# A decoder layer on one core: batch inputs loaded in another step, a product between V and scores, other last steps of self-attention, the last head's output taken by batch

## The chip, the cores and the metric

The kernel runs on one core of a Trainium2 chip. The time is the device time of one execution in microseconds (us); the median of several executions is compared. The engines are named as the profile names them: PE (TensorE, with its weight loads as PEld), DVE (VectorE), ACT (ScalarE), POOL (GpSimd) and SP (SyncE, which only issues DMAs here). A name with q, such as SPq, is an engine's queue of issued work.

## What is computed

One layer of a post-norm decoder in float32, on x of 8 batches x 256 tokens x 1024 features (16 tiles of 128 tokens):

```
x = layernorm(x + self_attention(x))              # 32 heads of 32, 8 key/value heads, rope, causal
x = layernorm(x + cross_attention(x, context))    # 32 heads of 128, 8 key/value heads, rope, mask
x = layernorm(x + gate(x) * memory(x))            # the last part
# memory: top 8 of 256 slots by a router, softmax over them, values through two small matrices
# gate: from the variance of each token (and the mean over all of them) and a small gelu network
```

The gate divides log(1 + variance) by its mean over all 2048 tokens. So the last part can be finished for no token before the second layernorm's input is there for every token.

## The kernel before

**Self-attention** (`self_attention`, line 147) runs 64 steps: s = 8 b + c for batch b and group c of four heads. The order of work on PE and POOL is the written one (`manual_schedule`, line 97); for the other engines and for DMAs issued by SP and ACT the framework's planner sets an order when the kernel is built, from the written order and its own idea of when each is ready. Each queue then runs strictly in its order, so that an instruction that waits holds up all that stand behind it. A step holds:

- `scores(s + 1)` (line 258), 16 matmuls of 32 rows (L267), whose results DVE reads with the mask (L284), ACT turns into softmax weights (L289, L295) and DVE transposes in blocks (L300, L304);
- `query(s + 2)` (L208), from the batch's input xT, and the rope on DVE (L218 to L221);
- in odd steps, for two steps at a time, `weighted` (line 316): the product of the weights and V in many 32 x 32 matmuls (L333), in two halves (`False`: 96 of them, `True`: 112), then four ACT copies to sa_oT (L343). Scores and weighted use the same two pairs of "sc" banks in PSUM, so scores of the next step wait for these copies;
- one of `others(s)`: keys and values of the next batch (c from 4 to 7), or the output projection of the batch before (`project_out`, L367, c from 0 to 3), and transposes of that batch's normalised tiles (`turn`, L391, c of 5 and 6), stored to x1T in DRAM;
- in steps 4 to 59 four `products`: the keys and values of the cross-attention, which do not depend on x, are made here.

Each such product is one of seven in a Strassen-Winograd scheme (`seven`, line 720): p1, p2, p6, p5, p3, p7, p4, eight matmul instructions each (L741, or L735 for values, which are turned). They read a quarter (512 tokens) of the context, or of x1T for queries, in blocks B11, B21, T3 (loaded as B12), B22 and the differences T1, T2, T3, T4 (`load_blocks`, line 621: loads L628, differences L632 to L635). p1 reads B11, p2 B21, p6 T2, p5 T1, p3 B22, p7 T3, p4 T4. Sums of the weights for these products are made on POOL in the self-attention (L417) and pass through DRAM.

All weights, the mask, the transposed tiles and some others share nine buffers ("w4", line 105). A load into one of them waits until its last reader is done. The batch inputs xT have two buffers (`load_x`, L162).

At the end, step 61 closes the early pool and opens the buffers of the cross-attention (`xa_early`, line 598): x1T of the first quarter, tables, keys and mask are loaded, and `mask_bias` (L679) turns the mask into what is added to scores. The first queries' seven products (`self.queries`) go into steps 62 and 63, two each, and behind the loop; those of the second pair between the last output projections.

**Cross-attention** (`cross_attention`, line 1022; only PE in written order) runs 128 heads H in four quarters q: transposes of head H (L877), scores of head H + 1 (L843), output products of the previous group of four heads (`xa_out`, seven again, L947), query products, and for each pair of heads the V product for each of two batches b (`xa_weighted`, L894, copies L902). `xa_combine` (L976) adds the sevens' parts to the residual. The memory part of the quarter before is fed in piece by piece (`self.fill`): `turn`, `project` (L1226), `query_turned` (L1236), `slot_weights` (L1243 to L1269), `weights_turned` (L1274), `mixed` (L1283).

**The tail** (`tail`, line 1408) follows the last head, whose group (G = 31) takes its output the plain way, `xa_out_plain` (L1002, 8 instructions for each half of a tile, then the layer norm). The last four tiles' memory parts, the mean variance, the gates and the 16 `final` (line 1362: two matmuls L1373, gate and add with sums on DVE L1376, the mean on POOL L1380 and L1381, squares on ACT L1384, the rest of the statistics on POOL L1385 to L1387) and their `norm` (L1394 or L1396, then the store) are interleaved by hand on PE.

The loop's middle, as it decides the order on PE:

```
if s % 2:
    weighted(s, False)
elif not first:
    one()
if s % 2 == 0 and s + 1 < last:
    scores(s + 1)
...
event()
one()
if s % 2:
    weighted(s, True)
    if s + 1 < last:
        scores(s + 1)
```

`one()` emits the next product of the step, `event()` a piece of the weights' sums.

Of the kernel before, what the change touches and what calls it, by code (L numbers as in the profile page):

```python
# [8 lines left out]
F32 = mybir.dt.float32  # L9
# [3 lines left out]
ALU = mybir.AluOpType  # L13
# [31 lines left out]
W4 = 9  # L45
# [25 lines left out]
class Layer:  # L71
# [16 lines left out]
    def run(self):  # L88
        nc = self.nc
        self.ident = self.const.tile([P, P], F32, name="ident")  # L90
        make_identity(nc, self.ident)
        self.neghalf = self.const.tile([P, 1], F32, name="neghalf")
        nc.gpsimd.memset(self.neghalf, -0.5)
        self.cos = self.const.tile([P, TQ], F32, name="cos")
        self.sin = self.const.tile([P, TQ], F32, name="sin")
        self.wsums, self.kT_d, self.v_d, self.tables_d = {}, {}, {}, {}
        with self.tc.manual_schedule(engines={PE, POOL}):
            self.self_attention()
        with self.tc.manual_schedule(engines={PE}):
            self.cross_attention()  # L100
            self.tail()

# [44 lines left out]
    def self_attention(self):  # L147
# [12 lines left out]
        def load_x(b):  # L160
            xTs[b] = ep.tile([P, KC, S], F32, name="xT", bufs=2)
            nc.sync.dma_start(out=xTs[b], in_=a["xT"][b])  # L162
# [344 lines left out]
        for s in range(last):  # L507
            b, c = divmod(s, KC)
            if c == 4:
                load_residual(b)  # L510
            if c == 6 and b + 2 < B:
                load_x(b + 2)
            if s == KV_BEGIN - 2:
# [84 lines left out]
    def xa_early(self):  # L598
# [13 lines left out]
        self.load_mask(0)  # L612
        self.mask_bias()

# [5 lines left out]

    def load_blocks(self, pool, name, src):


        nc = self.nc
        xb = {}
        for block, i, j in (("B11", 0, 0), ("B21", 1, 0), ("T3", 0, 1), ("B22", 1, 1)):
            xb[block] = pool.tile([P, 4, S], F32, name=name, bufs=7)
            nc.sync.dma_start(out=xb[block], in_=src[:, 4 * i : 4 * i + 4, j * S : (j + 1) * S])  # L628
        for block in ("T1", "T2", "T4"):
            xb[block] = pool.tile([P, 4, S], F32, name=name, bufs=7)  # L630

        nc.vector.tensor_tensor(xb["T1"], xb["T3"], xb["B11"], ALU.subtract)  # L632
        nc.vector.tensor_tensor(xb["T2"], xb["B22"], xb["T1"], ALU.subtract)
        nc.gpsimd.tensor_tensor(xb["T3"], xb["B22"], xb["T3"], ALU.subtract)
        nc.vector.tensor_tensor(xb["T4"], xb["B21"], xb["T2"], ALU.subtract)  # L635
        return xb

    def load_x1T(self, q):
        self.xb[q] = self.load_blocks(self.xp, "x1T", self.x1T_d[q])

    def xa_context(self, q):

        self.load_positions(q)
        self.cb = self.load_blocks(self.hp, "ctxT", self.a["ctxT"][q])

# [376 lines left out]
    def cross_attention(self):  # L1022
# [9 lines left out]
        for H in range(XA_STEPS):  # L1032
# [27 lines left out]
            def query():  # L1060
                if queries:
                    queries.pop(0)()
# [11 lines left out]
            for b in range(NB):  # L1074
                self.xa_turned(H, b)
            if H + 1 < XA_STEPS:
                self.xa_scores(H + 1, 0)
                if not waits:
                    query()
                self.xa_scores(H + 1, 1)  # L1080
            if i < 3:
# [23 lines left out]
            if i == 3:  # L1105
                if g == 0 and q:
                    self.xa_combine(q - 1, 0, True)
                if G == NQ * XA_KV - 1:
                    self.xa_combine(q, 0, False)
                    self.xa_combine(q, 1, False)  # L1110

# [251 lines left out]
    def final(self, t, x, wvu):  # L1363
# [5 lines left out]
        for half in range(2):  # L1369
# [9 lines left out]
            )  # L1379
        nc.gpsimd.tensor_tensor(nmean, sums[:, 0:1], sums[:, 1:2], ALU.add)  # L1380
        nc.gpsimd.tensor_scalar(nmean, nmean, -1.0 / E, None, ALU.mult)  # L1381

# [24 lines left out]

    def tail(self):
        nc = self.nc
        while self.fill:  # L1410
            self.next_fill()
        q = NQ - 1
        G = NQ * XA_KV - 1
        hid = self.uni.tile([P, QT, UNC], F32, name="w4", bufs=W4)
        tiles = [self.memory_tile(q * QT + tt, hid[:, tt, :]) for tt in range(QT)]
        norms = []
# [11 lines left out]
        def part(tt, i):  # L1428
            tiles[tt][i]()

        turn, project, query_turned, slot_weights, weights_turned, mixed = range(6)
        for t in range(8, NT - QT):
            self.load_x2(t, self.sp, "acc", 4)
        for tt in range(QT):
            for half in range(2):
                self.xa_out_plain(G, half, tt)
            if tt >= 2:
                part(tt - 2, turn)

# [7 lines left out]
        for i in range(2):  # L1447
            self.auxT.append(self.uni.tile([P, NT // 2 * P], F32, name="w4", bufs=W4))
            n = (NT // 2 - (QT if i else 0)) * P
            for half in range(2):  # L1450
# [3 lines left out]
                )  # L1454
        part(0, project)
        part(2, turn)
        part(1, project)
        part(0, query_turned)
        part(3, turn)
        lv = self.mean_log_variance()  # L1460
        part(2, project)
# [4 lines left out]
        part(1, slot_weights)  # L1466
        part(2, query_turned)
        finals(1)
        part(0, weights_turned)
        part(2, slot_weights)  # L1470
        part(3, query_turned)
        finals(1)
        part(0, mixed)
        part(1, weights_turned)
        part(3, slot_weights)
        self.memory_learned(hid, range(NT - QT, NT))
        finals(1)
        part(1, mixed)
        part(2, weights_turned)
# [5 lines left out]
        self.gates(lv, NT - QT, NT)  # L1485
        finals(NT - 5)
        for norm in norms:
# [91 lines left out]
```

## Time and profile before

| | |
|---|---|
| median of 3 runs (lowest, highest) | 3517.1 us (3503.24, 3520.21) |
| profiled execution: its time, its span | 3504.15 us, 3502.4 us |
| mean granted TensorE clock | 0.982 |
| busy: PE, PEld, DVE, ACT, POOL | 97%, 70%, 60%, 34%, 29% |
| self-attention loop, 60 to 1190 us: PE busy | 1091.6 us of 1130 |
| its end, 1190 to 1240 us: PE busy | 33.95 us of 50 |
| tail, 3440 us to the end: PE, DVE, ACT busy | 35.2, 40.69, 32.85 us of 63 |

The waits view lists, for one engine, the instruction that waited, what it waited for, the us in total, how often, and the longest. A timeline row has the start, the us that the merged instructions took, engine and line, the operation, out<-in by the program's names, shapes, xcount, and in brackets the idle time before it with what ended it. A row of the stretches has the length, each engine's busy time and count (PE, PEld, DVE, ACT, POOL), PEclk (the granted clock, 1 is full), the DMA share and GB/s.

### The profile page before, as it was taken

The numbers are of one execution on the slowest core, as the hardware profiler recorded it, in microseconds if no ns is written. First come the engines' busy times: TensorE is split into PE (matmuls) and PEld (weight loads), VectorE is DVE, ScalarE is ACT, GpSimd is POOL, SyncE is SP. The second block draws the span as 40 slices with busy tenths as digits, with TensorE's granted clock in tenths as the row PEclk, the third lists the DMA queues.
The fourth block names the chain that finished last, engine by engine and source line by source line (L and its number), as shares of the span: only waits on it lengthen the run. The fifth ranks groups of instructions, "written<-read, shape, count | busy, mean of one in ns | idle before, by whom it ended". The sixth has DMA issues, their size and how long they took to land.

```text
span 3502.4 us, 71117 instructions
## 1 busy us (share of the span) xinstructions
PE 3388.1 (97%) x27811; PEld 2459.2 (70%) x27811; DVE 2113.6 (60%) x5997; ACT 1201.2 (34%) x4030; POOL 1030.2 (29%) x1385
## 2 busy tenths in 40 slices
PE   7999999999999799999999999999999999999996
PEld 5777777787777567767776667677767766766753
DVE  4655665565555555566575665666575567566666
ACT  3434333343334423333223323333332333333224
POOL 4244655565665212111122111212111112121112
PEclk9999999999999899999999999999999999999997
DMA  8567777886877545344544334544434544444442
GB/s 291 192 218 261 272 255 256 278 273 216 299 256 252 184 160 160 126 146 135 157 145 153 129 127 140 167 136 148 137 127 135 159 153 145 133 131 134 130 142 96
DMA packets 269550, 626.36 MB, mean 179 GB/s; under 512 B 28960, under 2 KB 99760, under 8 KB 268192
## 3 DMA queue, kind: packets, MB, share of 16 engines
q1 hardware_dynamic: 194672, 441.00, 38.6%
q0 software_dynamic: 50032, 154.66, 13.6%
q10 hardware_dynamic: 24512, 26.15, 2.2%
q8 instruction: 221, 3.62, 0.4%
q14 instruction: 113, 0.93, 0.1%
HBM read 526.93 MB, written 94.77 MB: 178 GB/s over the span
## 4 chain that ended last, share of the span: by engine, by line
PE 71%; POOL 8%; issue 6%; DMA 6%; DVE 6%; ACT 2%; SPq 0%; POOLq 0%; ACTq 0%; DVEq 0%
PE mm L741 23%; PE mm L947 20%; PE mm L894 7%; PE sc L843 6%; PE mm L208 4%; POOL ws L417 3%; PE mm L735 3%; PE mm L367 2%; PE mm L1226 2%; DMA xa_wo_sums<-ws 2%; DMA xa_wq_sums<-ws 2%; PE sc L333 1%; PE sc L267 1%; POOL xa_wo_sums L466 1%; PE mm L1002 1%
## 5 line engine op out<-in xcount | busy, mean ns | idle before, releaser
L741 PE MATMUL mm<-x1T,w 128*128 128x256 f32 x3584 | 851.1, 381 | 5.0 <-DMA w<-in_xa_wq 3.8
L741 PEld LDWEIGHTS mm<-x1T,w 128*128 128x128 f32 x3584 | 676.3, 190 | 190.7 <-issue 87.7
L947 PE MATMUL mm<-w,xoS 128*128 128x512 f32 x992 | 449.2, 595 | 1.2 <-issue 1.2
L857 ACT ACTIVATE xatt<-xatt,nmax 128x256 f32<-128x256 f32 x512 | 257.2, 503 | 497.8 <-DVE nmax L852 488.6
L660 POOL DMA_DIRECT2D v<-v x256 | 151.2, 597 | 737.7 <-PE mm L894 617.8
L947 PE MATMUL mm<-w,xoT 128*128 128x512 f32 x744 | 338.2, 597 | 5.3 <-ACT xoT L902 4.1
L947 PEld LDWEIGHTS mm<-w,xoS 128*128 128x128 f32 x992 | 185.0, 190 | 194.2 <-issue 173.5
L208 PE MATMUL mm<-xT,w 128*128 128x256 f32 x1280 | 301.9, 392 | 10.2 <-DMA xT<-in_xT 10.2
L747 DVE TENSOR_TENSOR half<-mm,half 128x256 f32<-128x256 f32 x288 | 119.8, 416 | 287.0 <-PE mm L741 262.0
L208 PEld LDWEIGHTS mm<-xT,w 128*128 128x128 f32 x1280 | 244.3, 195 | 59.9 <-issue 23.7
L894 PEld LDWEIGHTS mm<-xat,v 32*128 32x128 f32 x8192 | 242.5, 187 | 51.0 <-issue 26.9
L913 POOL TENSOR_TENSOR xoS<-xoT 128x512 f32<-128x512 f32 x62 | 79.0, 1274 | 675.8 <-ACT xoT L902 675.5
L894 PE MATMUL mm<-xat,v 32*128 32x128 f32 x8192 | 267.5, 277 | 3.6 <-DVE acc L954 1.4
L289 ACT ACTIVATE att<-att,nmax 128x128 f32<-128x128 f32 (+1 forms) x512 | 225.4, 441 | 125.8 <-DVE nmax L284 120.6
L843 PE MATMUL sc<-kT,qT 128*128 128x256 f32 x1024 | 262.7, 380 | 0.0
L863 ACT ACTIVATE xatt<-xatt,rec 128x256 f32<-128x256 f32 x512 | 231.0, 498 | 86.6 <-DVE rec L861 85.3
L902 ACT COPY xoT<-mm 128x128 f32<-128x128 f32 x512 | 97.8, 276 | 468.9 <-PE mm L894 431.8
L417 POOL TENSOR_TENSOR ws<-ws 128x256 f32<-128x256 f32 x320 | 244.5, 764 | 26.6 <-DMA ws<-in_xa_wk 6.1
L747 DVE TENSOR_TENSOR raw<-mm,half 128x256 f32<-128x256 f32 x384 | 158.8, 414 | 153.0 <-PE mm L741 118.1
L947 PEld LDWEIGHTS mm<-w,xoT 128*128 128x128 f32 x744 | 138.7, 190 | 147.7 <-issue 126.8
L735 PEld LDWEIGHTS mm<-w,ctxT 128*128 128x128 f32 x1792 | 213.7, 197 | 24.9 <-issue 17.2
L735 PE MATMUL mm<-w,ctxT 128*128 128x128 f32 x1792 | 217.8, 282 | 11.0 <-DMA w<-xa_wv_sums 7.8
(229 smaller groups left out, 4861.1 us busy)
## 6 DMA issues: line engine op xcount, KB each, us to landing
w<-xa_wq_sums SPq DMA_DIRECT2D x128, 512.0 KB, 3.6
w<-xa_wo_sums SPq DMA_DIRECT2D x124, 512.0 KB, 3.6
w<-in_xa_wo SPq DMA_DIRECT2D x97, 512.0 KB, 4.0
w<-in_sa_wq SPq DMA_DIRECT2D x64, 512.0 KB, 7.6
sa_wo<-in_sa_wo SPq DMA_DIRECT2D x64, 512.0 KB, 6.0
w<-in_xa_wq SPq DMA_DIRECT2D x64, 512.0 KB, 3.5
v<-v POOLq DMA_DIRECT2D x256, 128.0 KB
w<-xa_wk_sums SPq DMA_DIRECT2D x32, 512.0 KB, 7.1
```

The source lines that it names most:

```text
L208: nc.tensor.matmul(ps[:, :S], lhsT=lhs[:, k, :], rhs=xT[:, k, :], start=(k == 0), stop=(k == KC - 1),)
L289: nc.scalar.activation(att[:, jj, lo:hi], att[:, jj, lo:hi], AF.Exp, bias=nmax[:, i : i + 1], scale=-1.0, accum_out=sums[:, i : i + 1],)
L417: nc.gpsimd.tensor_tensor(out, in0, in1, op)
L660: self.nc.gpsimd.dma_start(out=v[32 * i : 32 * i + 32], in_=rows)
L735: nc.tensor.matmul(ps[:, t * P : (t + 1) * P], lhsT=rhs[:, k, t * P : (t + 1) * P], rhs=w[:, k, :], start=(k == 0), stop=(k == 3),)
L741: nc.tensor.matmul(ps[:, :S], lhsT=w[:, k, :], rhs=rhs[:, k, :], start=(k == 0), stop=(k == 3))
L747: nc.vector.tensor_tensor(out, in0, in1, ALU.add)
L843: nc.tensor.matmul(sc[:, qt, :], lhsT=qT[:, q0 : q0 + P], rhs=kT[:, b * S : (b + 1) * S], start=True, stop=True,)
L857: nc.scalar.activation(att[:, qt, :], att[:, qt, :], AF.Exp, bias=nmax[:, qt : qt + 1], scale=-1.0, accum_out=sums[:, qt : qt + 1],)
L863: nc.scalar.activation(att[:, qt, :], att[:, qt, :], AF.Identity, bias=0.0, scale=rec[:, qt : qt + 1])
L894: nc.tensor.matmul(banks[i][:, :P], lhsT=v[rows, c, :], rhs=at[rows, c, :], start=(c == 0), stop=(c == BLOCKS - 1),)
L947: nc.tensor.matmul(ps, lhsT=oT[lhs][:, u, off + p * P : off + (p + 1) * P], rhs=w[:, u, :], start=(u == 0), stop=(u == 1),)
```

## The change

- The input xT of a batch is loaded two steps later: batch b + 1 at the end of step 8 b instead of batch b + 2 at the start of step 8 b + 6.
- In odd steps one of the four products moves from behind the next scores to between `weighted(s, True)` and those scores.
- Steps 62 and 63: four of the first seven query products behind the scores in step 62; in step 63 five products ahead of the V product (the other three, and two of the second pair's), one behind its first half. What is left of the second pair's first four comes right after the loop, and no product stands between the output projections. The mask's bias is made after the loop.
- `load_blocks` loads in the order B11, B12, B22, B21; T4 is made on POOL; T1 and T2 too for the first quarter of x1T.
- The last head calls the tail itself, with its left output product. The combine comes first, then the V product of batch 0, the outputs of its two tiles with their memory parts, and only then the V product of batch 1 and its tiles. The memory parts stand in another order, and one more final precedes the last gates.
- In `final` one DVE instruction makes the mean from the two sums, instead of two on POOL.

```diff
@@ self_attention
-            if c == 6 and b + 2 < B:
-                load_x(b + 2)
...
-            elif s > last - 3:
-                mine, self.queries = self.queries[:2], self.queries[2:]
+            elif s == last - 2:
+                mine, self.queries = self.queries[:4], self.queries[4:]
+            elif s == last - 1:
+                mine = self.queries + more[:3]
+                more = more[3:]
...
+            if s == last - 1:
+
+                for _ in range(5):
+                    one()
             if s % 2:
                 weighted(s, False)
-            elif not first:
+            elif not first and s < last - 2:
                 one()
...
             if s % 2:
                 weighted(s, True)
+                one()
                 if s + 1 < last:
                     scores(s + 1)
...
+            if b and c == 0 and b + 1 < B:
+                load_x(b + 1)
             if s + 3 < last:
                 load_query(s + 3)
...
             if s == last - 3:
                 early.close()
                 self.xa_early()
+                more = self.xa_query(1)
...
-        for part in self.queries:
-            part()
+        self.mask_bias()
+        more.pop(0)()
+        self.queries = more
         project_out(B - 1, 0)
-        queries = self.xa_query(1)
-        queries.pop(0)()
         project_out(B - 1, 1)
         load_out(B - 1, 1)
         self.xa_scores(0, 0)
         project_out(B - 1, 2)
         self.xa_scores(0, 1)
-        queries.pop(0)()
         project_out(B - 1, 3)
-        queries.pop(0)()
-        queries.pop(0)()
-        self.queries = queries
@@ xa_early
-        self.mask_bias()
@@ load_blocks
-        for block, i, j in (("B11", 0, 0), ("B21", 1, 0), ("T3", 0, 1), ("B22", 1, 1)):
+        for block, i, j in (("B11", 0, 0), ("T3", 0, 1), ("B22", 1, 1), ("B21", 1, 0)):
...
-        nc.vector.tensor_tensor(xb["T1"], xb["T3"], xb["B11"], ALU.subtract)
-        nc.vector.tensor_tensor(xb["T2"], xb["B22"], xb["T1"], ALU.subtract)
-        nc.gpsimd.tensor_tensor(xb["T3"], xb["B22"], xb["T3"], ALU.subtract)
-        nc.vector.tensor_tensor(xb["T4"], xb["B21"], xb["T2"], ALU.subtract)
+        engine.tensor_tensor(xb["T1"], xb["T3"], xb["B11"], ALU.subtract)
+        engine.tensor_tensor(xb["T2"], xb["B22"], xb["T1"], ALU.subtract)
+        self.nc.gpsimd.tensor_tensor(xb["T3"], xb["B22"], xb["T3"], ALU.subtract)
+        self.nc.gpsimd.tensor_tensor(xb["T4"], xb["B21"], xb["T2"], ALU.subtract)
...
+        engine = nc.vector if q else nc.gpsimd
+        self.xb[q] = self.load_blocks(self.xp, "x1T", self.x1T_d[q], nc.sync, engine)
@@ cross_attention
+            if H + 1 == XA_STEPS:
+                self.tail(outs)
+                return
@@ final
-        nc.gpsimd.tensor_tensor(nmean, sums[:, 0:1], sums[:, 1:2], ALU.add)
-        nc.gpsimd.tensor_scalar(nmean, nmean, -1.0 / E, None, ALU.mult)
+        nc.vector.tensor_scalar(nmean, sums[:, 0:1], sums[:, 1:2], -1.0 / E, ALU.add, ALU.mult)
@@ tail: the order on PE after the change
+        for part in outs + self.fill:
...
+            self.xa_combine(q, p, False)
...
+        self.xa_weighted(XA_STEPS // 2 - 1, 0)
         for t in range(8, NT - QT):
             self.load_x2(t, self.sp, "acc", 4)
...
+        out(0)
...
+        out(1)
+        part(0, turn)
+        part(0, project)
+        self.xa_weighted(XA_STEPS // 2 - 1, 1)
+        part(1, turn)
...
         part(1, project)
         part(0, query_turned)
+        out(2)
         part(0, slot_weights)
         part(1, query_turned)
+        out(3)
+        part(1, slot_weights)
+        part(2, turn)
+        part(2, project)
+        part(0, weights_turned)
+        lv = self.mean_log_variance()
+        part(3, turn)
+        part(1, weights_turned)
+        part(0, mixed)
         self.gates(lv, 0, NT - QT)
+        part(2, query_turned)
         part(3, project)
+        part(1, mixed)
         finals(1)
         part(2, slot_weights)
         part(3, query_turned)
         self.memory_learned(hid, range(NT - QT, NT))
         finals(1)
+        part(3, slot_weights)
+        finals(2)
         part(2, weights_turned)
         finals(1)
         part(2, mixed)
...
-        finals(NT - 5)
+        finals(NT - 6)
```

More of the change, by code (lines that the diff above doesn't have):

```diff
@@ L100, in run @@
             self.cross_attention()
-            self.tail()
     def weights(self, shape, src, dtype=F32):
@@ L619, in xa_psum, with load_blocks @@
         self.banks = [mm, mm, more]
-    def load_blocks(self, pool, name, src):
-        nc = self.nc
+    def load_blocks(self, pool, name, src, queue, engine):
         xb = {}
-        for block, i, j in (("B11", 0, 0), ("B21", 1, 0), ("T3", 0, 1), ("B22", 1, 1)):
+        for block, i, j in (("B11", 0, 0), ("T3", 0, 1), ("B22", 1, 1), ("B21", 1, 0)):
             xb[block] = pool.tile([P, 4, S], F32, name=name, bufs=7)
-            nc.sync.dma_start(out=xb[block], in_=src[:, 4 * i : 4 * i + 4, j * S : (j + 1) * S])
+            queue.dma_start(out=xb[block], in_=src[:, 4 * i : 4 * i + 4, j * S : (j + 1) * S])
         for block in ("T1", "T2", "T4"):
             xb[block] = pool.tile([P, 4, S], F32, name=name, bufs=7)
-        nc.vector.tensor_tensor(xb["T1"], xb["T3"], xb["B11"], ALU.subtract)
-        nc.vector.tensor_tensor(xb["T2"], xb["B22"], xb["T1"], ALU.subtract)
-        nc.gpsimd.tensor_tensor(xb["T3"], xb["B22"], xb["T3"], ALU.subtract)
-        nc.vector.tensor_tensor(xb["T4"], xb["B21"], xb["T2"], ALU.subtract)
+        engine.tensor_tensor(xb["T1"], xb["T3"], xb["B11"], ALU.subtract)
+        engine.tensor_tensor(xb["T2"], xb["B22"], xb["T1"], ALU.subtract)
+        self.nc.gpsimd.tensor_tensor(xb["T3"], xb["B22"], xb["T3"], ALU.subtract)
+        self.nc.gpsimd.tensor_tensor(xb["T4"], xb["B21"], xb["T2"], ALU.subtract)
         return xb
     def load_x1T(self, q):
-        self.xb[q] = self.load_blocks(self.xp, "x1T", self.x1T_d[q])
+        nc = self.nc
+        engine = nc.vector if q else nc.gpsimd
+        self.xb[q] = self.load_blocks(self.xp, "x1T", self.x1T_d[q], nc.sync, engine)
     def xa_context(self, q):
         self.load_positions(q)
-        self.cb = self.load_blocks(self.hp, "ctxT", self.a["ctxT"][q])
+        self.cb = self.load_blocks(self.hp, "ctxT", self.a["ctxT"][q], self.nc.sync, self.nc.vector)
     def load_tables(self, q):
@@ L1075, in cross_attention @@
                 self.xa_turned(H, b)
[L1076 to L1080, printed above, removed]
+            if H + 1 == XA_STEPS:
+                self.tail(outs)
+                return
+            self.xa_scores(H + 1, 0)
+            if not waits:
+                query()
+            self.xa_scores(H + 1, 1)
             if i < 3:
@@ L1107, in cross_attention @@
                     self.xa_combine(q - 1, 0, True)
-                if G == NQ * XA_KV - 1:
-                    self.xa_combine(q, 0, False)
-                    self.xa_combine(q, 1, False)
     def memory_setup(self):
@@ L1406, in load_x2, with tail @@
         self.nc.sync.dma_start(out=self.xs[t], in_=self.x2[t])
-    def tail(self):
+    def tail(self, outs):
         nc = self.nc
-        while self.fill:
-            self.next_fill()
+        for part in outs + self.fill:
+            if part:
+                part()
         q = NQ - 1
         G = NQ * XA_KV - 1
-        hid = self.uni.tile([P, QT, UNC], F32, name="w4", bufs=W4)
-        tiles = [self.memory_tile(q * QT + tt, hid[:, tt, :]) for tt in range(QT)]
+        for p in range(2):
+            self.xa_combine(q, p, False)
         norms = []
@@ L1431, in tail, with out @@
         turn, project, query_turned, slot_weights, weights_turned, mixed = range(6)
+        def out(tt):
+            for half in range(2):
+                self.xa_out_plain(G, half, tt)
+        self.xa_weighted(XA_STEPS // 2 - 1, 0)
         for t in range(8, NT - QT):
             self.load_x2(t, self.sp, "acc", 4)
[L1434 to L1438, printed above, removed]
+        out(0)
+        hid = self.uni.tile([P, QT, UNC], F32, name="w4", bufs=W4)
+        tiles = [self.memory_tile(q * QT + tt, hid[:, tt, :]) for tt in range(QT)]
+        out(1)
[3 more added lines that the diff above has]
+        part(1, turn)
         wvu = self.uni.tile([P, 512], F32, name="w4", bufs=W4)
@@ L1454, in tail @@
                 )
-        part(0, project)
-        part(2, turn)
         part(1, project)
         part(0, query_turned)
-        part(3, turn)
-        lv = self.mean_log_variance()
-        part(2, project)
+        out(2)
         part(0, slot_weights)
         part(1, query_turned)
+        out(3)
[7 more added lines that the diff above has]
+        part(0, mixed)
         self.gates(lv, 0, NT - QT)
+        part(2, query_turned)
         part(3, project)
-        part(1, slot_weights)
-        part(2, query_turned)
+        part(1, mixed)
         finals(1)
-        part(0, weights_turned)
         part(2, slot_weights)
         part(3, query_turned)
[L1472 to L1475, printed above, removed]
         self.memory_learned(hid, range(NT - QT, NT))
         finals(1)
-        part(1, mixed)
+        part(3, slot_weights)
+        finals(2)
         part(2, weights_turned)
```

## The prediction

> **What bounds the kernel now.** I read the table of busy time by stretch first. TensorE (PE) is busy 3388.1 of 3502.4 us, and between 1310 and 3390 us, the cross-attention, PE idles 11 us in 2080. What can be won lies in three places: the self-attention loop (60 to 1190 us: 1091.6 busy of 1130), its end (1190 to 1240: 33.95 of 50) and the tail (3440 to the end: 35.2 of 63). For these I read the waits, then the timelines. In the loop, waits of PE (us in total, times, longest), then of SP's DMA queue:
>
> ```profile
> PE sc L267 <- ACT sa_oT L343: 8.4, 7, 1.2
> PE mm L735 <- DMA w<-xa_wv_sums: 7.8, 2, 5.8
> PE mm L741 <- DMA w<-xa_wk_sums: 3.4, 1, 3.4
> ```
> ```profile
> SPq L162 <- PE mm L208: 133.5, 6, 32.3
> ```
> The first is the scores of an even step, waiting until ScalarE (ACT) has copied the attention outputs out of the "sc" banks. The last is the load of the next batch's xT: it heads SP's queue for up to 32.3 us, until PE has made the last query from the old xT, and the weight loads of the products stand behind it. One instance of each on PE:
>
> ```profile
> 539.91 1.26 PE L267 MATMUL sc<-sa_kT,sa_qT 32*128 32x128 f32 x16 [1.17 <-ACT sa_oT L343]
> 541.10 9.04 PE L735 MATMUL mm<-w,ctxT 128*128 128x128 f32 x64
> 550.07 0.94 PE L267 MATMUL sc<-sa_kT,sa_qT 32*128 32x128 f32 x16
> ...
> 576.17 3.75 PE L741 MATMUL mm<-ctxT,w 128*128 128x256 f32 x8 [3.43 <-DMA w<-xa_wk_sums]
> ```
> and the clock after the first (PEclk is the column after the engines):
>
> ```profile
> 541.00:545.00 4.00, 4.00 (x22) 3.90 (x21) 2.62 (x18) 3.65 (x16) 3.34 (x5) 0.57 0.67 256
> 545.00:549.00 4.00, 4.00 (x39) 4.00 (x38) 2.39 (x9) 2.68 (x10) 0.00 (x0) 1.00 0.30 98
> ```
> At the loop's end, on PE and on VectorE (DVE):
>
> ```profile
> 1205.43 1.89 PE L741 MATMUL mm<-x1T,w 128*128 128x256 f32 x8
> 1219.73 1.32 PE L333 MATMUL sc<-at,sa_v 32*32 32x128 f32 x4 [12.41 <-DVE at L300]
> 1222.34 2.81 PE L333 MATMUL sc<-at,sa_v 32*32 32x128 f32 x92 [1.29 <-DVE at L300]
> 1225.08 3.10 PE L741 MATMUL mm<-x1T,w 128*128 128x256 f32 x8
> ```
> ```profile
> 1207.26 1.22 DVE L632 TENSOR_TENSOR x1T<-x1T 128x1024 f32<-128x1024 f32 x1 [5.11 <-DMA x1T<-x1T]
> ...
> 1211.12 2.76 DVE L635 TENSOR_TENSOR x1T<-x1T 128x1024 f32<-128x1024 f32 x1
> ```
> The last V product waits for the softmax transposes (L300), which stand behind block differences that wait for a load. In the tail, ACT:
>
> ```profile
> 3491.49 1.15 ACT L1384 ACTIVATE xat<-res,f_stats 128x1024 f32<-128x1024 f32 x1 [2.07 <-POOL f_stats L1381]
> 3494.89 1.15 ACT L1384 ACTIVATE xat<-res,f_stats 128x1024 f32<-128x1024 f32 x1 [2.15 <-POOL f_stats L1381]
> ```
> Each square waits for a mean that GpSimd (POOL) makes only after the tile before is done.
>
> **The change, part by part.** The profiled execution took 3504.15 us (span 3502.4). It lies 13 us under the median of the three runs (3517.1), near the lowest (3503.24). The sum is made against 3504.15.
>
> (a) *A product between V and scores.* The 28 odd steps 5 to 59 get one; no work is added. In 21 of them the scores start at once, but take 1.27 us until the next matmul (619.89 to 621.16) where scores behind a product take 0.87 (550.07 to 550.94): 21 x 0.40 = 8.4. In seven PE idles, 8.4 in all, and the scores then still take 1.19 (539.91 to 541.10): 7 x 0.32 = 2.2. A product lasts 1.7 to 1.9 us, longer than the wait of 1.2, so both go: 19. Behind five of the seven (227, 388, 541, 859, 1173 us) the granted clock halves for 3.4 us: the 64 matmuls at 541.10 took 9.04 us where 48 took 5.62 at full clock, so 7.5 were due: 1.5 each, 7.5 in all. Ceiling 26.5. What may come back: the next scores have one product less ahead of them. DVE has read the scores 3.5 us after they start (619.89, last read ends 623.4), and the next come 6.8 us after in the tightest steps, 5.1 then: not late. I take 20, and 8 as the low end (only the plain waits go, half-clock windows fall elsewhere).
>
> The row says that 1.1 us of idleness in a stretch of thin 32-row matmuls is followed by half clock. The Trainium skill, "TensorE: Matmul & The Clock Gate" (What's actually happening), has the clock halve after an idle window of about 3.4 us, which 1.1 us does not fill; by that alone the 7.5 us would be nothing. The measured windows decide.
>
> (b) *The xT load moves from step 8b+6 to 8b+8.* SP then meets it after the last query of the old batch (made in step 8b+5), so it waits for nothing, and it is used four steps (some 70 us) later. What goes: the PE waits at 264, 576 and 890 us, 2.0 + 3.4 + 5.8 = 11.2, each just behind this load. Behind them the clock halved too: by matmul spacing 2.7, 4.3 and 1.9 us (the 8 at 576.17 took 3.75 against 1.89). Ceiling 20. In the third, SP had been held by context loads before, and by this one for 4.6 only. Its 1 MB now goes out beside other loads, at a mean DMA share of 0.7 to 0.8. I take 14, low end 4.
>
> (c) *The end of self-attention.* The trace has no such order, so by hand. Gone: 12.41 + 1.29, and 1.83 before the first product; at half clock 0.86 (2.81 against 1.95 for as many) and 1.2 (3.10 against 1.89): 17.6. The transposes no longer stand behind L632 to L635, since for the first quarter all four differences go to POOL, and nine products (15.6 us) stand before the last V product instead of two. New waits: scores 63 no longer has a product ahead and waits for the reads of scores 62, 2.1; the second product now needs the block loaded last (the fourth load landed at 1209.3; PE is there at 1205.6), 3.8 (scores 63, a turn and one product after 1202); the third needs weights issued at 1209.07 that land 3.5 us later, 1.4. POOL needs 2.36 to 3.27 us a difference, four in series from 1205 to about 1216; the last is needed at 1219: hidden, unless they run 1 us longer each. Last, the products that stood between the final output projection (ended 1269.5) and the transposes of its second tile are used up; that tile was normalised at 1274.1, so PE waits 3.6. New: 10.9; net 6.7. I take 6; ends -3 (a half clock behind the new gap, weights late) and 13.
>
> (d) *The tail.* Mean on DVE (one op of 0.15 to 0.2 us) for two on POOL (0.19 + 0.22 to 0.7), and no longer behind the last tile's POOL chain. From 3459.5 to 3491.6 twelve tiles passed, 2.7 us each. DVE needs 2 x 0.67 + 0.17, and 0.73 for ten of sixteen norms: 2.0, with the rest of the memory work about 2.2: 12 x 0.5 = 6. The wait of 4.1 us at 3447 for slot weights (L1274) goes, as two tiles are through by then, and 1.7 before the last V product; against them, project directly behind turn three times (about 0.45 each, a 0.68 us copy against 0.43 us of transposes), V of batch 0 directly before the output that reads it (0.9), and two slots' transposes and mixes (2.4) ahead of the first final. Much of this cancels; I take 5, ends -5 and 11.
>
> (e) *The rest*: block order, a difference on POOL instead of DVE in later quarters (2.4 us against 1.2 to 1.95; ready at least 12 us before its use at 1746), the mask's bias later (0.65 us): nothing, hidden under PE work; uncovered, each is its own 1 to 3 us.
>
> Sum: 20 + 14 + 6 + 5 = 45; 3504.15 - 45 = 3459. All low ends: 8 + 4 - 3 - 5 = 4, 3500; all high ends: 26.5 + 20 + 13 + 11 = 70.5, 3434.
>
> **Rivals.**
> - *The load is planned ahead again* (the change doesn't do what it says): SP's order is the planner's, and it now holds xT as far ahead as before. For: it waited six times, so it was not placed where it is written. Against: it stood behind all loads of earlier steps. (b) is 0: 3473.
> - *The waits change their name*: with less cover, PE waits for weights or softmax at the next place, in (a) and (b) both; weight loads wait 405 us in SP's queue for buffers. Low ends, (c) and (d) at 3 and 0: 3489.
> - *The half clock stays*: it does not hang on the 1.1 us waits but on the thin matmuls around them, and two of the seven waits (702, 1019 us) had none behind them. (a) loses 5.5 of its 20, 3465. The page of the Trainium skill cited under (a) would have it so.
> - *The tail is late*: the output weights share nine buffers with four later tiles and queue behind loads that waited 12 us for the accumulators; PE reaches the last output 4 us earlier than it did. (d) is -12: 3476.
> - *Slower*: the softmax chain becomes the bound. Odd scores' transposes end 9 to 13 us after the scores, V follows after 13 to 17, and in the tightest step 0.35 us are left. If the product put first delays its DVE and ACT work by more than 3 us in each of 28 steps, V waits 3 us each time: +84, and with the 45 gained 3543. It decides from 1.6 us a step. For: 1.7 us later scores, and four of the products bring 2 us of rope on DVE ahead. Against: margins of 3 us and more nearly everywhere.
>
> **How the numbers follow.** Forecast 0.52, waits renamed 0.18, planned ahead 0.12, half clock stays 0.08, late tail 0.06, slower 0.04. The predicted time is 3459. The range is 3434 to 3500: it spans all terms' ends and every rival but the slow one, and has room for an execution 13 us higher, as two of the three runs were. The measurement tells about 0.5% (17.6 us) from no change: faster by more 0.88, within 0.08 (part of the renamed waits, all low ends), slower 0.04.
>
> **What would show it.** (a) PE's wait L267 on L343 near 0, 0.9 us for even scores, no half clock near 541. (b) The wait of L162 under 10 us, no PE waits on sums weights near 264, 576, 890. (c) No wait over 5 us between 1190 and 1240, one of 3 to 4 us at the last transposes. (d) Squares no longer waiting for POOL, about 2.2 us a tile. It is wrong if SP still waits 20 us or more at the xT load, if L333 waits more than 20 us in the loop, or if the tail is longer than 122 us from 3380.

## The result, and the profile after

The changed kernel took **3480.6 us** (median of five runs, 3477.3 to 3483.1) beside 3508.7 us for the kernel before (five runs, 3503.2 to 3520.2): a ratio of 0.991, with a 95% interval of 0.9888 to 0.9932. The profiled execution took 3477.49 us, with a span of 3475.7 and a mean granted clock of 0.986. By the spans the change took away 26.7 us (28.0 by the medians), where 45 were forecast. The time lies inside the range and 21.6 us above the predicted 3459.

Two executions are best compared at points that both pass. Four stretches: the loop, up to the start of scores 62; the end of self-attention, up to the cross-attention's scores of head 10; the cross-attention, up to the scores of the last head; the tail.

| span in us | loop | end | cross-attention | tail | whole |
|---|---|---|---|---|---|
| before | 1198.6 | 202.6 | 1966.3 | 134.8 | 3502.4 |
| after | 1179.7 | 193.3 | 1971.2 | 131.5 | 3475.7 |
| difference | -18.9 | -9.3 | +4.9 | -3.3 | -26.7 |

PE's waits in the loop of the changed kernel (60 to 1179 us), then SP's at the load of xT:

```profile
PE mm L738 <- DMA w<-xa_wv_sums: 9.5, 4, 5.8
PE sc L332 <- DVE at L299: 5.7, 5, 3.0
PE mm L744 <- DMA w<-xa_wk_sums: 3.6, 1, 3.6
...
PE mm L704 <- DVE raw L750: 3.1, 1, 3.1
```
```profile
SPq L161 <- PE mm L207: 119.9, 5, 29.3
```
The wait of scores for the copies of sa_oT (8.4 us before) is gone. But SP still waits at xT, 119.9 us where it was 133.5, and PE's waits on weight sums, which were to go with it, have grown from 11.2 to 13.1 us. The waits of PE that the view lists for the loop make 34.5 us, against 35.9: what went in one place came in others. The timeline of PE at the step shown before, with the product (530.99) between V and the scores, and then a stretch around it:

```profile
529.67 1.39 PE L332 MATMUL sc<-at,sa_v 32*32 32x64 f32 x112
530.99 2.05 PE L738 MATMUL mm<-w,ctxT 128*128 128x128 f32 x16
532.97 0.94 PE L266 MATMUL sc<-sa_kT,sa_qT 32*128 32x128 f32 x16
533.84 5.62 PE L738 MATMUL mm<-w,ctxT 128*128 128x128 f32 x48
539.39 0.94 PE L266 MATMUL sc<-sa_kT,sa_qT 32*128 32x128 f32 x16
...
565.71 2.50 PE L744 MATMUL mm<-ctxT,w 128*128 128x256 f32 x8 [3.65 <-DMA w<-xa_wk_sums]
```
```profile
525.00:545.00 20.00, 20.00 (x253) 16.65 (x252) 12.14 (x54) 10.03 (x41) 12.11 (x17) 1.00 0.73 250
```
Scores of an even step now take 0.87 us up to the next matmul, and PEclk is 1.00 over the whole stretch, where it was 0.57 in the 4 us behind these scores before; the weights at 565.71 are as late as they were at 576. From 60 us to scores 62 the granted clock stood at half for 17 windows of 3.4 us before and for 12 after. By the spacing of like matmuls in them, this cost some 23 us before and some 16 after (an estimate). So of the loop's 18.9 us, 1.4 come from the listed waits and some 7 from the clock. The other 10.5 are about what the prediction had for the pace of the 28 scores, 8.4 and 2.2.

The end of self-attention on PE, and GpSimd's four differences:

```profile
1182.09 0.80 PE L266 MATMUL sc<-sa_kT,sa_qT 32*128 32x128 f32 x4 [1.09 <-DVE nmax L283]
...
1191.12 3.31 PE L744 MATMUL mm<-x1T,w 128*128 128x256 f32 x8 [1.85 <-DMA x1T<-x1T]
1195.31 12.32 PE L744 MATMUL mm<-x1T,w 128*128 128x256 f32 x56 [0.89 <-DMA w<-xa_wq_sums]
1207.57 1.49 PE L332 MATMUL sc<-at,sa_v 32*32 32x128 f32 x96
...
1249.71 1.09 PE L390 MATMUL mm<-ident,res 128*128 128x128 f32 x8 [1.29 <-DVE res L376]
```
```profile
1187.41 2.36 POOL L633 TENSOR_TENSOR x1T<-x1T 128x1024 f32<-128x1024 f32 x1 [8.58 <-ACT att L294]
...
1194.46 2.81 POOL L636 TENSOR_TENSOR x1T<-x1T 128x1024 f32<-128x1024 f32 x1
```
The V product (1207.57) waits for nothing, where it waited 12.41 and 1.29 us. Each of the four new waits that were forecast came in its place and was smaller (1.09 and 0.32 for the scores, 1.85, 0.89, 1.29); one of 0.5 us for ACT's copies (1212.82) was not forecast. In the tail, ACT's squares of the last tiles now wait for DVE's mean instead of GpSimd's, half as long (1.05 and 0.94 for 2.07 and 2.15):

```profile
3463.71 1.15 ACT L1385 ACTIVATE xat<-res,f_stats 128x1024 f32<-128x1024 f32 x1 [1.05 <-DVE f_stats L1382]
...
3465.89 1.15 ACT L1385 ACTIVATE xat<-res,f_stats 128x1024 f32<-128x1024 f32 x1 [0.94 <-DVE f_stats L1382]
```

### The profile page after: what moved, and what is told of

It is laid out like the page before. It is cut to its first block, busy times and chain, and to the rows that moved or that the text cites. A ratio compares the mean times of both kernels' runs of the same rounds, so it can differ in the third digit from the quotient of the medians.

```text
span 3475.7 us, 71117 instructions
## 1 busy us (share of the span) xinstructions
PE 3373.5 (97%) x27811; PEld 2447.3 (70%) x27811; DVE 2114.2 (61%) x6003; ACT 1202.3 (35%) x4030; POOL 1047.0 (30%) x1363
## 3 DMA queue, kind: packets, MB, share of 16 engines
q0 software_dynamic: 50032, 154.66, 13.7%
## 4 chain that ended last, share of the span: by engine, by line
PE 86%; DVE 6%; ACT 3%; DMA 3%; POOL 2%; issue 1%; SPq 0%; POOLq 0%; DVEq 0%; ACTq 0%
PE mm L744 26%; PE mm L950 19%; PE mm L207 7%; PE mm L897 7%; PE mm L366 6%; PE sc L846 6%; PE mm L738 5%; PE sc L332 2%; PE mm L1228 2%; PE sc L266 1%; ACT att L288 1%; PE mm L236 1%; DMA w<-xa_wv_sums 1%; ACT att L294 1%; PE mm L1005 1%
## 5 line engine op out<-in xcount | busy, mean ns | idle before, releaser
L750 DVE TENSOR_TENSOR half<-mm,half 128x256 f32<-128x256 f32 x288 | 119.9, 416 | 300.6 <-PE mm L744 268.3
```

What stands on the lines that cost most here:

```text
L750: nc.vector.tensor_tensor(out, in0, in1, ALU.add)
```

## The experiments

Where an edit is small, the stretches of the profiled execution tell more than the medians, but they come from one execution each. In the changed kernel and in the five runs that leave its loop alone, or move only T4 or the written line of the load there, the loop took 1176.6 to 1181.8 us, so a difference under 5 us there shows nothing. The nine profiles that share the changed end have 191.8 to 195.2 us for it, the eight that share the changed tail 131.4 to 134.5. Each ratio is to executions of the kernel before that were taken beside that run, so ratios and medians of different runs do not line up to the last few us.

### The xT load on GpSimd's queue

```diff
-            nc.sync.dma_start(out=xTs[b], in_=a["xT"][b])
+            (nc.gpsimd if b > 1 else nc.sync).dma_start(out=xTs[b], in_=a["xT"][b])
```

> The changed kernel (3480.6 us) with one edit: the loads of xT for batches 2 to 7 are issued on GpSimd's queue, whose order is the written one, and no longer on SP's. Theory 'the load still heads SP's queue': the change moved the line and not the load, so SP still waited 119.9 us at it and the weights behind it came late (PE waits of 13.1 us on weight sums, half clock behind them 7.5 us). Here SP's wait is gone, the waits on weight sums fall below 3 us and the half-clock stretches near 263, 567 and 877 us go: 15 to 20 us faster than the changed kernel, 3461 to 3466. Rival 'the weights are late anyway' (SP waits for free buffers, or the 1 MB transfer itself is in the way): SP's wait moves to the weight loads, PE's waits on sums stay above 9 us, and the time is within 4 us of 3480.6. Second rival: issuing on GpSimd or the later arrival of xT costs PE a wait at the next keys (line 236), and the time is above 3480.6.

It took 3469.0 us (3458.7 to 3471.4), ratio to before 0.9873 (0.9849 to 0.9897), 11.6 us less than the changed kernel by the medians. The loop took 1170.2 us, 9.5 less. PE's waits in it:

```profile
PE mm L704 <- DMA w<-in_xa_table,pos_u: 6.0, 4, 3.1
...
PE mm L738 <- DMA w<-xa_wv_sums: 1.9, 1, 1.9
```
The waits on sums fell from 13.1 to 1.9 us, and near 263 and 567 us the granted clock is 1.00 (it was 0.57 and 0.50). The loads went out from 159.1 to 940.7 us, where the line stands; in the changed kernel SP issued them at 114.1 to 868.9 us, like before (115.5 to 885.6). So the mechanism was right and the change does not set it off. The gain fell short of the 15 to 20 us expected, and one reason is a new wait: GpSimd issued the gather of the rope tables when PE was already there (6.0 us, with half clock behind it at 897 us).

### The product between V and scores, taken out and alone

```diff
                 weighted(s, True)
-                one()
                 if s + 1 < last:
```

> The changed kernel without the product between the V product and the next scores (it goes back behind them). Theory: of the 19 us that the self-attention loop gained up to the last scores, about 12.4 are the pace of 28 odd steps (0.44 us each), 8.4 are the seven waits on the copies of sa_oT, 5 are half-clock stretches, and 7 were given back as other short waits. So this kernel loses 15 to 20 us: 3496 to 3501, and the loop again shows about 8 us of waits of scores on sa_oT copies. Rival 'the gain in the loop came from the moved load or from the block order': the time stays within 5 us of 3480.6. Rival 'waits only change their name': scores wait on the copies again, but the softmax waits of the V product fall by as much, and it loses the pace alone, 8 to 12 us: 3489 to 3493.

> The kernel before with that product alone, nothing else of the change. If the parts add up, it gains in the loop what the loop gained with all parts, 15 to 20 us, and nothing at the end of self-attention, in the cross-attention and in the tail: 3489 to 3494 beside 3508.7. Rival: the moved load shares the loop's gain, and this one gains only 8 to 12.

Without the product the changed kernel took 3500.8 us (3491.8 to 3508.6), ratio 0.9964 (0.9943 to 0.9985): 20 us lost. Its profiled execution was the longest of its runs, with a loop of 1213.4 us. The scores waited for the copies seven times again, 8.4 us in all:

```profile
543.23 1.97 PE L266 MATMUL sc<-sa_kT,sa_qT 32*128 32x128 f32 x16 [1.17 <-ACT sa_oT L342]
545.13 8.31 PE L737 MATMUL mm<-w,ctxT 128*128 128x128 f32 x64
```
```profile
544.00:548.00 4.00, 4.00 (x29) 3.35 (x26) 2.41 (x17) 2.83 (x13) 3.50 (x5) 0.62 0.65 252
```
and behind five of these seven waits the half clock is back (from 226, 390, 544, 711 and 1032 us). Added alone to the kernel before, the product gave 3484.1 us (3481.2 to 3489.6), ratio 0.9928 (0.9908 to 0.9948). Its stretches are 1173.7, 203.0, 1967.8 and 134.8: the loop gained 24.9 us, and the end and the tail nothing. Alone, this one line gains nearly as much as the whole change. It also keeps the long wait at the end (the timeline of PE in that kernel):

```profile
1194.87 1.32 PE L333 MATMUL sc<-at,sa_v 32*32 32x128 f32 x4 [11.37 <-DVE at L300]
```

### The load written where it was

```diff
+            if c == 6 and b + 2 < B:
+                load_x(b + 2)
...
-            if b and c == 0 and b + 1 < B:
-                load_x(b + 1)
```

> The changed kernel with the xT load written where it was (step 8b+6, batch b+2). Theory: SP's order is the planner's, which puts the load at its estimate of the old buffer's release, wherever the line stands; so SP waits some 120 to 135 us at it again, PE's waits on weight sums stay near 13 us, and the time is within 5 us of 3480.6. Rival 'the moved line costs the loop something': the kernel before with the product alone had reached the last scores 6 us earlier (1173.7 us) than the changed kernel (1179.7), and the moved line is the largest other edit in the loop; then the last scores come near 1174 and the time near 3475. Second rival, the forecast's: the move is worth 14 us after all; then the time is near 3494.

3480.3 us (3478.5 to 3486.9), ratio 0.9938 (0.9916 to 0.9959), and SP waits 122.2 us at xT. Moving the line back changes nothing that can be measured. The first rival fell too: the loop took 1181.8 us and not 1174.

### T4 on DVE again

```diff
-        self.nc.gpsimd.tensor_tensor(xb["T4"], xb["B21"], xb["T2"], ALU.subtract)
+        engine.tensor_tensor(xb["T4"], xb["B21"], xb["T2"], ALU.subtract)
```

> The changed kernel with the difference T4 on DVE again for all but the first quarter of x1T (and for the context), the order of the block loads left as changed. Theory: the cross-attention gave back 4.9 us, 2.0 near 1700, 0.5 near 2262 and 2.45 near 2808, because GpSimd's two differences run there beside the rope on DVE (its first multiplication took 2.15 us for 0.68), and the V product then waited for DVE twice and ran at half clock. With T4 on DVE these 4.9 us come back: 3476, and the multiplication takes 0.7 us. Rival 'the block loaded last is what is late': T4 has to wait for B21, DVE is held by it, and the cross-attention is as slow as in the changed kernel or slower.

3473.8 us (3467.5 to 3478.4), ratio 0.9893 (0.9871 to 0.9915), 6.9 us less than the changed kernel by the medians, though the intervals of the two ratios overlap. The cross-attention took 1966.9 us for 1971.2. In the changed kernel this is how it loses there; DVE, GpSimd and PE around 1695 us:

```profile
1694.64 2.15 DVE L717 TENSOR_TENSOR qT<-raw,cos 128x512 f32<-128x512 f32 x1
```
```profile
1693.89 2.35 POOL L636 TENSOR_TENSOR x1T<-x1T 128x1024 f32<-128x1024 f32 x1 [4.68 <-PE sc L846]
```
```profile
1698.98 0.48 PE L897 MATMUL mm<-xat,v 32*128 32x128 f32 x2 [0.76 <-DVE acc L957]
1700.19 3.68 PE L897 MATMUL mm<-xat,v 32*128 32x128 f32 x58 [0.72 <-DVE acc L957]
```
The rope's multiplication takes 2.15 us instead of 0.68 and ends 0.55 us after GpSimd's difference (1696.79 and 1696.24). The sums behind it on DVE are late, and PE waits twice and runs its V product at half clock (58 matmuls in 3.68 us instead of 2.05). With T4 on DVE, one wait of 0.72 us is left at this place, the 58 matmuls behind it take 2.05 us, and the timeline of DVE reads:

```profile
1693.36 1.21 DVE L636 TENSOR_TENSOR x1T<-x1T 128x1024 f32<-128x1024 f32 x1
1694.49 0.68 DVE L717 TENSOR_TENSOR qT<-raw,cos 128x512 f32<-128x512 f32 x1
```
Not all of the 4.9 us is T4's, though. Over all profiles the cross-attention took 1967.7 to 1971.3 us with T4 on GpSimd (six kernels, mean 1969.7) and 1964.1 to 1970.4 without (eight, mean 1966.7): some 3 us.

T4 is in the way in the loop as well. In the changed kernel, DVE, GpSimd and PE near 360 us:

```profile
362.81 0.81 DVE L376 TENSOR_SCALAR res<-res,ln_mv,ln_rstd 128x1024 f32<-128x1024 f32 x1 [7.18 <-POOL ln_rstd L131]
363.54 0.42 DVE L750 TENSOR_TENSOR raw<-mm,half 128x256 f32<-128x256 f32 x1
```
```profile
357.60 2.35 POOL L635 TENSOR_TENSOR ctxT<-ctxT 128x1024 f32<-128x1024 f32 x1
359.90 2.34 POOL L636 TENSOR_TENSOR ctxT<-ctxT 128x1024 f32<-128x1024 f32 x1
362.20 0.58 POOL L131 TENSOR_TENSOR ln_rstd<-ln_ve,neghalf 128x1 f32<-128x1 f32 x1
```
```profile
364.01 1.30 PE L704 MATMUL mm<-ident,w 128*128 128x128 f32 x6 [3.15 <-DVE raw L750]
```
GpSimd does T4 ahead of one short power for a layer norm. DVE stands 7.18 us at the norm that needs it; a read of PE's bank stands behind that norm; PE waits 3.15 us for the bank and then runs at half clock. With T4 on DVE, DVE's wait is 3.87 us and PE's 0.9. The loop as a whole (1179.5 us) does not show it: it is smaller than what executions differ by.

### The old order of the last steps, and the differences on DVE

The first restores the last steps and the products behind the loop, the second only the engine:

```diff
-            elif s == last - 2:
-                mine, self.queries = self.queries[:4], self.queries[4:]
-            elif s == last - 1:
-                mine = self.queries + more[:3]
-                more = more[3:]
+            elif s > last - 3:
+                mine, self.queries = self.queries[:2], self.queries[2:]
...
```
```diff
-        engine = nc.vector if q else nc.gpsimd
+        engine = nc.vector
...
-        self.nc.gpsimd.tensor_tensor(xb["T4"], xb["B21"], xb["T2"], ALU.subtract)
+        engine.tensor_tensor(xb["T4"], xb["B21"], xb["T2"], ALU.subtract)
```

> The changed kernel with the old order of the last steps: two products each in steps 62 and 63, the rest where they stood before, the mask's bias in step 61. The differences of the first quarter stay on GpSimd. From scores 62 to the xa scores of head 10 the kernel before took 202.7 us and the changed one 193.3. Theory 'the order did it' (nine products ahead of the last V product cover the softmax, and no last turn waits): it loses 8 to 10 us, 202 us for that stretch, 3490. Rival 'the engine did it': the V product had waited 12.4 us because its transposes stood behind the differences on DVE; with these on GpSimd the old order does without most of that wait, and the stretch takes 193 to 197 us.

> The changed kernel with all differences on DVE but T3, as before, in every quarter (the other side of the last question). If the order alone matters, the nine products cover the transposes even behind the differences: the stretch from scores 62 to head 10 takes 193 to 195 us, and with T4 on DVE the cross-attention gains its 4.9 us: 3474 to 3477. If the engine matters, the V product waits for transposes again, 5 to 12 us: 3480 to 3488.

The old order took 3486.0 us (3478.2 to 3490.7), ratio 0.9943 (0.9923 to 0.9964), with 198.6 us for the end; its V product still waited 6.9 us for its transposes, half of the 13.7 before. The differences on DVE took 3473.7 us (3466.5 to 3482.3), ratio 0.9911 (0.9877 to 0.9945), with 195.6; its V product waited for no transposes. So the order alone covers the whole of that wait, and the engine alone half of it. Between 202.6 and 193.3 us, the order is worth 5.3 us where GpSimd makes the differences. The engine's 2.3 us where the order is new are hardly more than what this stretch differs by from profile to profile, and they are not saved at the V product.

### The mean in the tail

```diff
-        nc.vector.tensor_scalar(nmean, sums[:, 0:1], sums[:, 1:2], -1.0 / E, ALU.add, ALU.mult)
+        nc.gpsimd.tensor_tensor(nmean, sums[:, 0:1], sums[:, 1:2], ALU.add)
+        nc.gpsimd.tensor_scalar(nmean, nmean, -1.0 / E, None, ALU.mult)
```
and the reverse of it in the kernel before.

> The changed kernel with the mean of the finals on GpSimd again, two instructions for one on DVE. From the last scores to the end the kernel before took 134.8 us and the changed one 131.4. Theory of the forecast: the mean was worth 0.5 us a tile; squares wait for GpSimd again, the twelve last finals go back from 2.48 to about 2.7 us or more each, and the stretch takes 135 to 138 us. Rival 'the norm waits anyway': in the changed kernel DVE waits 1.0 to 1.4 us at every odd norm for GpSimd's statistics, so these bound the finals already, and a mean on GpSimd costs 1 us in all at most: 131 to 133 us.

> The kernel before with the mean of the finals made by one DVE instruction, nothing else of the change. In the changed kernel, putting the mean back on GpSimd cost 4.8 us of the tail (from 131.5 to 136.3 us after the last scores). Theory: the mean is worth about as much in the old order, so that the tail of before falls from 134.8 to 129 to 131 us, and the new order of the tail is worth nothing or costs 1 to 2 us. Rival: in the old order the tail is held by the waits that the reorder took away (4.1 us for slot weights), the mean alone gives under 2 us, and the two parts need each other: 133 to 135 us.

With the old mean the changed kernel took 3481.7 us (3479.8 to 3485.4), ratio 0.9930 (0.9894 to 0.9967), and its tail 136.2 us; by the time alone it cannot be told from the changed kernel. The mean alone in the kernel before took 3498.3 us (3492.0 to 3508.9), ratio 0.9971 (0.9951 to 0.9991), and its tail 130.1. In these four tails the mean gives 4.7 us in either order (134.8 to 130.1, 136.2 to 131.5), and the new order costs 1.4. But the changed tail differs by 3 us between profiles (132.5 us in the mean of eight), so the mean's worth is some 4 to 5 us, and of the order only the sign is likely. All of the tail's gain is one instruction.

### Put together

Both edits that helped (the load on GpSimd's queue, T4 on DVE); then the gather issued earlier and the norm one tile later; then the old tail as well:

```diff
+            left = len(products)
+            context = KV_BEGIN <= s < KV_END and left and left % (XA_KV // 2 * 14) == 0
+            if context:
+                self.load_positions(NQ - left // (XA_KV // 2 * 14))
             event()
...
-        self.load_positions(q)
+        if not q:
+            self.load_positions(q)
...
-                if len(norms) > 2:
+                if len(norms) > 3:
```

> The changed kernel with both edits that helped: xT loads on GpSimd's queue and T4 on DVE. Theory: the two costs are apart in place (the load near 264, 570 and 880 us; T4 near 350 us and in the cross-attention), so the gains add: 11.6 from the load and 6.9 from T4 by their medians, 3462 us; the stretch from the xa scores of head 10 to the last scores takes 1966 to 1967 us. Rival: GpSimd is lighter without T4, or the loop is bound by another thing now (the table gather, 6.0 us of PE waits in the run with the load alone), and the sum is short of it by more than 5: above 3467.

> The same with two edits more. The gather of the rope tables is issued before the step's weight sums on GpSimd instead of behind them, and a final's norm is written three tiles behind it instead of two. Theory: PE's waits on the gathered tables (6.0 us and a half-clock stretch near 897 us) go, 6 to 8 us in the loop; DVE's waits for GpSimd's statistics in the finals (8.0 us in the changed kernel) go, and the tail from the last scores falls from 131.5 to 125 to 128. Together 3450 to 3456. Rival: the tail is held by DVE's and ACT's own work or by the last tile's chain, so the lag gives under 2 us, and the sums delayed by the gather make weight waits; then 3459 to 3465.

> The fastest kernel so far (3450.4 us, tail 128.3) with the last head and the tail in the order of before; the mean stays on DVE and the norm three tiles behind. Theory: the new order costs what the two tails with the new mean differ by (131.5 against 130.1), so the tail falls to 126 to 128 us and the time is 3449 or a little less. Rival: with the norm's wait gone the slot weights are late, and the old order pays its 4.1 us: tail 130 to 133, time 3452 to 3456.

The first took 3454.1 us (3452.7 to 3456.0), ratio 0.9843 (0.9823 to 0.9862), 8 us less than the two gains added. Its loop took 1158.6 us: with 2.35 us less on GpSimd for each quarter of the context, the gather came in time, and PE's wait on it fell from 6.0 to 0.9 us. The second took **3450.4 us** (3448.5 to 3452.8), ratio 0.9833 (0.9813 to 0.9853). Its loop is the same (1159.0): the gather's wait is gone, but waits on rotated queries rose by 3 us. Its tail fell from 132.6 to 128.3 as DVE's waits for GpSimd's statistics fell from 8.2 to 1.6 us. DVE's waits in the tail, in the first and the second:

```profile
DVE acc L1395 <- POOL f_stats L1388: 2.8, 2, 1.4
DVE x1T L1395 <- POOL f_stats L1388: 2.3, 2, 1.1
DVE res L1395 <- POOL f_stats L1388: 1.9, 2, 1.0
...
DVE xoT L1395 <- POOL f_stats L1388: 1.2, 1, 1.2
```
```profile
DVE res L1400 <- POOL f_stats L1393: 1.4, 2, 0.7
...
DVE acc L1400 <- POOL f_stats L1393: 0.2, 1, 0.2
```
The third has a tail of 125.0 us, the shortest, so that the old order of the tail looks cheaper here too, and the wait for slot weights that its rival feared came back (3.4 us) without deciding. It took 3452.3 us (3445.2 to 3455.4), ratio 0.9828 (0.9805 to 0.9850): by the time it cannot be told from the second.

## Why the prediction was right, and where it was wrong

**The direction and the main cause (a) were right; its size was too low.** 20 us were forecast for the product; alone it gave 24.9 us in the loop, near the ceiling of 26.5. The three parts are all there: the waits on the copies, the pace, and the half clock behind those waits. In the changed kernel the loop gained only 18.9. The missing 6 us are little more than the 5 by which executions of the loop differ. One cost is seen, the norm behind T4 near 360 us (2.2 us more of PE's wait than with the product alone). The written place of the load and T4's engine changed nothing in the loop's total (1181.8 and 1179.5 us), and the new order of the block loads was not tried alone. The rest stays open.

On the clock the rows decided. In the changed kernel no half clock follows the scores that had waited, though the thin matmuls are still there; without the product it came back behind five of the seven waits. Two of the seven had none behind them in either kernel, and not the same two (702 and 1019 us before, 868 and 1186 without the product), so a wait of 1.2 us does not set it off every time, and what decides stays open. The Trainium skill's rule in "TensorE: Matmul & The Clock Gate" (What's actually happening), a halved clock after an idle window of about 3.4 us, would by itself have made the waits of 1.2 us harmless; here the measurement says otherwise. The length of each half-clock stretch in the loop does agree with that section: 3.4, 6.8 or 10.2 us, whole windows.

**(b) failed.** The step that fell is "SP then meets it after the last query of the old batch (made in step 8b+5), so it waits for nothing". It took the written place of a DMA for its place in the queue. Yet the line had stood behind that query before as well, at the start of step 8b+6, and SP had waited there six times: the rows on record spoke for the rival. SP's order is the planner's, which put the load 45 to 72 us ahead of where it is written. This was the rival with chance 0.12, and (b) gave 0 instead of 14. By the prediction's own sign, SP waiting 20 us or more at this load, the part is wrong. What the step said of the cause held: with the load really late, the waits on sums fell to 1.9 us.

**(c) was right and too low**: 9.3 us for 6, inside its ends. The forecast's new waits made 10.9 us; 1.4, 1.85, 0.89 and 1.29 were measured, 5.4 together. The last turn waited less than forecast because PE ran two blocks of scores and a product between the two turns. The half clock that the low end feared did come (the products at 1186 and 1191 us took 2.7 and 3.3 us for 1.9), so the balance is better than the 6.7 summed there by 2.6 us, and not by the 5.5 that the waits were smaller.

**(d) was near in sum, 3.3 us for 5, in a stretch that differs by 3 from profile to profile.** The mean gave 4.7 of the 6. The last finals came every 2.4 us (3446.58 to 3465.78 for eight), not 2.2, because DVE then waited 1.2 to 1.4 us at each odd norm for GpSimd's statistics, which the step did not count. The items of the reorder add up to a gain of about 1 us; by taking 5 in all the step allowed a loss of 1, and 1.4 were lost in this comparison. The wait for slot weights fell only from 4.1 to 2.3 us, and new waits came on PE, up to 2.9 us.

**(e), "nothing", was wrong**: some 3 us in the cross-attention over all profiles, 4.9 in this execution, and a wait of 3 us in the loop. The differences are ready long before their use, as the step said. It overlooked what stands beside and behind them: an engine that is off the path held up two that were on it.

With measured terms the sum is 24.9 for the product, less 6.0 taken back in the loop, 0 for the load, 9.3 at the end, less 4.9 in the cross-attention, 3.3 in the tail: 26.6, against 26.7 between the spans. That it closes proves little, since the four stretches make up the span. That the time fell into the range is owed in part to its width of 66 us, which held every rival but the slow one: without (b) the same sum gives 3473. It was luck that (a) alone and (c) came out larger, by 4.9 and 3.3 us, against what (e) and the loop took back. The slow rival did not show. The V product's waits on its transposes in the loop rose by about 1 us only.

## What to carry to other kernels

Find out who orders a queue before pricing a moved line: compare the time at which the transfer is issued with the step where it is written, and if they lie far apart, moving the line may move nothing, as here, while an engine with a fixed order can take the load over. A wait of one microsecond among thin matmuls can cost more than its length, and one independent product put in front of it can return all of it. Before an elementwise operation goes to an idle engine, look at what short operation stands behind it there and what the neighbouring engine runs at that moment.

## What the runs showed of the hardware

- DVE's multiplication of two tiles took 2.15 us instead of 0.68 when GpSimd's subtraction had started 0.75 us before it, and ended 0.55 us after it, less than the 0.68 that it takes alone: this reads as held until the other was done, and not as slowed. The Trainium skill, "SBUF — State Buffer" (SBUF: two separate sides), says the same: the two share a port pair that one instruction holds to its end. Here 1.5 us on DVE added 0.8 us to PE's waits (1.48 for 0.72), and 1.6 more through the clock.
- Half clock followed waits of 1.2 us where the work around them was 32-row matmuls, behind five of seven in the kernel before and in the one without the product. In the cross-attention's V product it followed 1.48 us of waits in two pieces (0.57 of full speed from 1700 to 1704 us), and did not follow a single wait of 0.72 us at the same place in the run with T4 on DVE.
